# Grouping of destination tiles, and when routed rows are scattered, in a two-layer graph and expert kernel

## The chip, the cores and the metric

The kernel runs on one core of a Trainium2 chip. A core has engines that each work through their own queue of instructions in order: PE (matrix products; its weight loads are listed as PEld), DVE (elementwise and reductions), ACT (elementwise with functions from a table, and copies), POOL (elementwise, and here the issuer of indirect DMAs) and SP (which only issues DMAs). They wait for each other by semaphores. The metric is the time of one execution on the device, in microseconds (us).

## The reference

The input is x, 3125 nodes of 256 features, and 50000 edges sorted by destination. Two layers follow, each a graph step and a mixture of experts, every one on a layernorm of x and added to x:

```
x = x + gnn0(layernorm(x))        # [x, x of one neighbour] @ W.T + b
x = x + experts0(layernorm(x))    # best 2 of 8, relu, hidden 1024
x = x + gnn1(layernorm(x))
x = x + experts1(layernorm(x))    # best 2 of 8, gelu, hidden 256
```

The part that matters here is the second layer. Its graph step is

```
t1  = feat @ W1
msg = (t1[src] + (feat[src] * feat[dst]) @ W2) / sqrt(out_deg[src] * out_deg[dst])
agg = segment_sum(msg, dst)
e   = leaky_relu(where(in_count > 0, t1 + agg, 0) + b, 0.01)
gnn1 = e / max(norm(e), 1e-12)
```

and its experts are, with the two best of a softmax over eight router scores, their weights scaled to sum to one,

```
out = tokens + sum over e of combine[:, e] * (gelu(tokens @ w1[e] + b1[e]) @ w2[e] + b2[e])
```

## The kernel before

Nodes are held in SBUF as T = 25 tiles of 128 rows (the last has 53), in the array X. They are two halves, tiles 0 to 13 and 14 to 24. For the experts, the rows of a half are sent to the sets of their two experts: in half 0 every expert has room for four tiles of rows, in half 1 for three. A set that overflows has extra sets, a branch that does not run here.

**Graph step of layer 1 (to_the_end, L1604 and following).** Edges are turned earlier into 25 tables of counts, one for each destination tile, in memory (atab). The neighbour sums of a group of destination tiles are then a dense product over all 25 source tiles. Groups are listed in `fours`: (0,4), (4,8), (8,12), (12,16), (16,19), (19,22), (22,25). For a group g there is

- `load(t)` (L1615): SP loads the counts of one tile;
- `begin(g)` (L1790): reserves the sums in PSUM, by turns under two names, and transposes the features of the group (turned_rows, L1639 to L1649);
- `product(g, i0, i1)` (L1775): ACT casts the counts from bytes (L1782), PE makes 100 products (L1786), four for each source tile;
- `end(g)` (L1796): two tiles at a time, DVE adds and multiplies the sums with the features (both_rows, L1652 to L1661), and then finish_steps is run for each tile.

**finish_steps (L1664)** makes eight products of a tile with W1 and W2 (L1672), three DVE operations (L1677 to L1679) and a sum of squares on ACT (L1681). The results of several tiles are gathered up to the end of a *span* of up to five tiles: (0,5), (5,10), (10,14), (14,19), (19,24), (24,25). At the last tile of a span come unit_steps (square root on ACT L1578, reciprocal, update of X, L1584) and score_steps (L918): layernorm statistics (L526 to L529), normed rows (L533), which go to `kept` in half 0 and to a buffer `xn5` in half 1, POOL's addition of the normed rows to X (L1588), transposes on PE (L935), a copy on ACT (L937), the router's products (L942), the scores' copy (L944), and for half 1 a store of the rows issued from ACT's queue (L946; the last span from SP's). `xn5` has one buffer; the single tile of the last span has its own, `xn1`. Half 0's last span is followed by route_steps: it ranks the scores, and gives every row its two places in the sets.

**Half 1: place_steps (L1700).** A span of half 1 gets its places as soon as it is scored, from running counts of each set (rank, two small products L1726 and L1727, DVE work), and is scattered to the sets by two indirect DMAs per tile on POOL (L1754). For the span (14,19) this is run in `end`; for the other two it is run beside the experts.

**Half 0: dispatch (L1759).** The rows in `kept` are scattered to the sets (table xtab) by two indirect DMAs per tile on POOL, 28 in all (L1765). It is called for two tiles at a time, after each of the tiles 14 to 20 is finished; ahead of each pair of tiles, DVE copies the places (L1762), and this copy is held in program order:

```
place = state["place"][:, :, t0:t1]
tc.keep_in_program_order(nc.vector.tensor_copy(place, routed2[0].at[:, :, t0:t1]))
```

**Order of the work.** Up to the experts a planner of the framework orders each engine's queue: of what its own cost estimate has ready it takes what is first in the program. A copy held in program order stays behind the DVE instruction traced just before it. The experts (L983) are in an order written out by hand: 16 sets, of which the first eight are half 0's. For each set SP loads the rows (L1037) and the weights (L972 to L980); PE transposes rows (L1061), DVE copies them (L1062); PE makes the hidden layer (L1088), ACT its gelu (L1092); PE makes the outputs (L1102), DVE adds a bias (L1107), POOL scatters them (L1111). The rows of the first two sets are loaded first, then the weights; the rows' load waits for all 28 scatters of half 0, since they write one table. At 11 points of a set of half 0 (10 in half 1), called slots, generators "beside" are moved on by one step. One is `beside_third` (L1830): it finishes and scores the last tile (24), places the spans (19,24) and (24,25), and then routes half 1; only after that are half 1's rows loaded. With finish and score of tile 24 and the two placings, 35 steps stand ahead of that routing.

**Memory.** The buffers of the experts lie where those of the graph step were: the weights of the first sets over the casted counts (`wide`), the transposed rows and the hidden layer over `kept` and over the buffers of route and place; the rows of the second set over a `wide` buffer.

Of the kernel before, what the change touches and what calls it, by code (L numbers as in the profile page):

```python
# [12 lines left out]
I32 = mybir.dt.int32  # L13
# [5 lines left out]
P = 128  # L19
D = 256  # L20
N = 3125
T = (N + P - 1) // P
# [26 lines left out]
HALVES = ((0, 14), (14, T))  # L49
# [31 lines left out]
def groups(n, size, first=0):  # L81
    return [(a, min(a + size, n)) for a in range(first, n, size)]


def run(steps):

    while True:
        try:
            next(steps)
        except StopIteration as end:  # L90
            return end.value
# [19 lines left out]
def gnn_ffn_kernel(ctx: ExitStack, tc: tile.TileContext, x, src_a, src_d, dst_d, dst_row,  # L111
                   gW, gb, fWg, fbg, fW1, fb1, fW2, fb2,
                   hW1, hW2, hb, rW, mw1, mb1, mw2, mb2, out):
    nc = tc.nc
# [7 lines left out]
    def bank(shape, dtype, tag, bufs=2):  # L122
        return psum.tile(shape, dtype, tag=tag, name=tag, bufs=bufs)
# [233 lines left out]
    with tc.tile_pool(name="edges", bufs=2, reuse_waits="tile") as ep:  # L357
# [68 lines left out]
        last = ep.tile([P, 2, T], F32, bufs=1)  # L426
# [66 lines left out]
        last = last[:, 0]  # L493
# [456 lines left out]
    def alone(dma, table, fresh=False):  # L950

        group = f"{table.name}{fresh}"
        tc.declare_no_dep(dma.ins, group=group, reason="other rows of the table")
        tc.add_to_no_dep_group(group, dma.ins)
# [371 lines left out]
    with tc.tile_pool(name="ffn", bufs=2, reuse_waits="tile") as fp:  # L1326
# [7 lines left out]
        with tc.tile_pool(name="gnn", bufs=2, reuse_waits="tile") as gp:  # L1334
# [27 lines left out]
            rp = gp_route.enter_context(tc.tile_pool(name="route", bufs=1, reuse_waits="tile"))  # L1362
# [212 lines left out]
    def unit_steps(emb, sq, t0, t1):  # L1575
        n = t1 - t0
        yield
        nc.scalar.activation(sq[:, :n], sq[:, :n], AF.Sqrt)  # L1578
        yield
        yield  # L1580
        nc.vector.tensor_scalar(sq[:, :n], sq[:, :n], 1e-12, None, OP.max)
        nc.vector.reciprocal(sq[:, :n], sq[:, :n])
        for t in range(t0, t1):
            nc.vector.scalar_tensor_tensor(X[:, t, :], emb[:, t - t0, :], sq[:, t - t0, :],  # L1584
                                           X[:, t, :], OP.mult, OP.add)
# [18 lines left out]
    def to_the_end():  # L1604


        routed2 = [Routed(True, 3, tag=("tr", 2)), Routed(True, by_expert=True)]
# [4 lines left out]
        gp = finishing.enter_context(tc.tile_pool(name="prod", bufs=1, reuse_waits="tile"))  # L1612
        sp = finishing.enter_context(tc.tile_pool(name="score2", bufs=1, reuse_waits="tile"))
        with tc.tile_pool(name="ahead2", bufs=2, reuse_waits="tile") as ap2:
            def load(t):  # L1615
                if t % 8 < 2:
                    at[t] = at[t % 8]
                elif t % 8 < 6:
                    at[t] = ap.tile([P, T, P], U8, name="at")
                else:  # L1620
                    at[t] = ap2.tile([P, T, P], U8, name="at2")
                nc.sync.dma_start(out=at[t].rearrange("p i d -> p (i d)"), in_=atab[t])

            for t in range(2, 8):
# [1 line left out]
                    with tc.tile_pool(name="comb1", bufs=2, reuse_waits="tile") as cp:  # L1626
                        run(combine_and_split(1, cp))
                load(t)
            spans = [g for a, b in HALVES for g in groups(b, 5, a)]
            state = {}  # L1630

            some_deg = gp.tile([P, T], F32, name="some_deg")
# [19 lines left out]
            def both_rows(t0, t1, sums, c0, featT):  # L1652

                n = (t1 - t0) * P if t1 < T else (t1 - t0) * P - P // 2
                both = gp.tile([P, 2, KD, 2 * P], F32, name="both", bufs=2)
                if t1 == T:
                    nc.vector.memset(both[:, :, :, n:n + P // 2], 0.0)
                for k in range(KD):
                    s, f = sums[k][:, c0:c0 + n], featT[:, k].rearrange("p t l -> p (t l)")[:, :n]
                    nc.vector.tensor_add(both[:, 0, k, :n], s, f)  # L1660
                    nc.vector.tensor_mul(both[:, 1, k, :n], s, f)  # L1661
                return both

            def finish_steps(t, both, i):  # L1664
                t0, t1 = next(g for g in spans if g[0] <= t < g[1])
                if t == t0:
                    state["emb"] = gp.tile([P, 5, D], F32, name="emb", bufs=1)
                    state["sq"] = gp.tile([P, 5, 1], F32, name="sq", bufs=2)
                po = bank([P, 2, D], F32, "y")
                for w, Wt in enumerate((hW1t, hW2t)):  # L1670
                    for k in range(KD):
                        nc.tensor.matmul(po[:, w, :], both[:, w, k, i * P:(i + 1) * P], Wt[:, k, :],  # L1672
                                         start=(k == 0), stop=(k == KD - 1))
                yield
                yield
                emb, junk = state["emb"][:, t - t0, :], gp.tile([P, D], F32, name="junk", bufs=2)
                nc.vector.scalar_tensor_tensor(junk, po[:, 1, :], some_deg2[:, t:t + 1], hbt, OP.mult, OP.add)  # L1677
                nc.vector.scalar_tensor_tensor(emb, po[:, 0, :], some_deg[:, t:t + 1], junk, OP.mult, OP.add)
                nc.vector.scalar_tensor_tensor(emb, emb, 0.01, emb, OP.mult, OP.max)  # L1679
                yield  # L1680
                nc.scalar.activation(junk, emb, AF.Square, accum_out=state["sq"][:, t - t0, :])  # L1681
                if t < t1 - 1:
                    return
                yield from unit_steps(state["emb"], state["sq"], t0, t1)
                h = int(t0 >= HALVES[1][0])
                if t0 == HALVES[h][0]:
                    state["pl"] = gp.tile([P, HALVES[0][1], NE], F32, name="pl", bufs=2)
                queue = nc.scalar if t1 < T else nc.sync
                xn = yield from score_steps(sp, h, t0, t1, state["pl"], rWt, tabs2[h][0], plus_normed,
                                            state["kept"][:, t0:t1, :] if h == 0 else None, queue)  # L1690
                if h == 1:
                    due.append((t0, t1, xn))
                if h == 0 and t1 == HALVES[0][1]:
                    with tc.tile_pool(name="route2", bufs=1, reuse_waits="tile") as rp:
                        run(route_steps(routed2[0], rp, 0, state["pl"][:, :HALVES[0][1]], 2))
                    state["place"] = gp.tile([P, 2, t1], I32, name="place")

            due = []

# [58 lines left out]

            def dispatch(t0, t1):  # L1759

                place = state["place"][:, :, t0:t1]
                tc.keep_in_program_order(nc.vector.tensor_copy(place, routed2[0].at[:, :, t0:t1]))  # L1762
                for t in range(t0, t1):
                    for i in range(2):
                        alone(nc.gpsimd.indirect_dma_start(  # L1765
                            out=tabs2[0][0], in_=state["kept"][:, t, :], in_offset=None,
                            out_offset=bass.IndirectOffsetOnAxis(ap=place[:, i, t - t0:t - t0 + 1], axis=0)),
                            tabs2[0][0])

            state["kept"] = ap2.tile([P, HALVES[0][1], D], F32, name="kept", bufs=1)  # L1770
            chunks = [g for a, b in HALVES for g in groups(b, 3, a)]
            fours = groups(16, 4) + groups(T, 3, 16)
            sums, featT = {}, {}

            def product(g, i0, i1):  # L1775
# [20 lines left out]
            def end(g):  # L1796
                t0, t1 = fours[g]
                for a, b in groups(t1, 2, t0):
                    both = both_rows(a, b, sums[g], (a - t0) * P, featT[a])
                    for t in range(a, b):  # L1800
                        if t == T - 1:
                            return both
                        run(finish_steps(t, both, t - a))
                        if due and t < T - 2:
                            with tc.tile_pool(name="place", bufs=1, reuse_waits="tile") as rp:
                                run(place_steps(rp, *due.pop()))
                        first = 2 * (t - HALVES[1][0])
                        if 0 <= first < HALVES[0][1]:
                            dispatch(first, first + 2)

            begin(0)
            begin(1)
            product(0, *HALVES[0])
            product(1, *HALVES[0])
            product(0, *HALVES[1])
            end(0)
            product(1, *HALVES[1])
            end(1)
            for g in range(2, len(fours)):
                for t in range(*fours[g]):  # L1820
                    if t >= 8:
                        load(t)
                begin(g)
                product(g, 0, T)
                last = end(g)

        aheads.close()
        fp = aheads.enter_context(tc.tile_pool(name="ffn2", bufs=3, side="right", reuse_waits="tile"))

        def beside_third():  # L1830
            yield from finish_steps(T - 1, last, 0)
            with tc.tile_pool(name="place", bufs=1, reuse_waits="tile") as rp:
                for one in due:
                    yield from place_steps(rp, *one)
            finishing.close()
            with tc.tile_pool(name="route3", bufs=1, reuse_waits="tile") as rp:
                yield from route_steps(routed2[1], rp, 1, None, 2, state["scores"])
# [319 lines left out]
```

## Time and profile before

| what | us |
|---|---|
| median of three runs | 1002.73 |
| the three runs | 1002.85, 1001.3, 1002.73 |
| profiled execution | 999.52 |
| its span, first to last instruction | 997.7 |
| last product L1786 ends | 812.8 |
| first expert product L1088 starts | 844.53 |
| third expert's L1088 starts | 869.79 |

The profile is of one execution. Its span lies between the first and the last instruction of the engines; the mean granted clock of PE over it is 0.957 of full speed. It lists, in this order: busy time of each engine with its share of the span and its number of instructions; busy tenths in forty slices (24.9 us each); DMA queues; the chain that ended last; the groups of instructions that cost most; DMA issues. A trace behind it can be asked for busy times in any stretch, and for one engine's timeline: start, duration, engine and line, operation, output<-inputs, shapes, count, and in brackets how long the engine had stood idle before, and on whose work. The costliest lines of the page in the second layer:

```
L1786 PE MATMUL sa<-wide,parts 128*128 128x512 f32 (+2 forms) x200 | 72.4, 365 | 2.4 <-ACT wide L1782 2.4
L1786 PE MATMUL big<-wide,parts 128*128 128x512 f32 (+1 forms) x300 | 71.7, 387 | 0.3 <-ACT wide L1782 0.3
L1786 PE MATMUL sb<-wide,parts 128*128 128x512 f32 (+2 forms) x200 | 71.9, 363 | 0.0
L1782 ACT CAST wide<-at 128x384 fp32r<-128x384 uint8 (+1 forms) x225 | 95.0, 485 | 42.0 <-PE sb L1786 21.5
```

A line of a group has the number of instructions, their busy time in us and the mean ns of one, and then the idle time of the engine just before them and what ended most of it. Busy times of PE overlap, since products are pipelined: from start to start a 512-wide product of L1786 takes 0.215 us.

### The profile page before, as it was taken

Reading aid. Unit: us, or ns where it says so; the run is one execution under the profiler, and the core shown is the slowest. Engines: PE = TensorE matmul, PEld = TensorE weight load, DVE = VectorE, ACT = ScalarE, POOL = GpSimd, SP = SyncE. Lnnn points to the kernel's source line nnn. Section 1 sums busy time; section 2 is a strip of 40 time slices with the busy share of each in tenths; the row PEclk is TensorE's granted clock in tenths of the full one; section 3 lists DMA queues with packets and bytes.
Section 4 is the critical chain, followed back from the end, with each engine's and each line's share of the span. In section 5 each row is a group of like instructions: output and inputs, shape, how many; then the busy total and the mean of one; then the engine's idle time right before and its main releaser. Section 6 shows DMA issues by size and latency. Waiting matters only on the chain. (4 is left out here: it accounts for less than half of the span.)

```text
span 997.7 us, 13976 instructions
## 1 busy us (share of the span) xinstructions
PE 875.3 (88%) x4819; PEld 653.5 (66%) x4819; DVE 595.2 (60%) x1585; ACT 413.1 (41%) x970; POOL 332.9 (33%) x338
## 2 busy tenths in 40 slices
PE   4778579998999999999999998899999974799880
PEld 3666446664766576777777776778889963566660
DVE  8966883773555555665566307452648771685553
ACT  2872421221126655666632236655455630412110
POOL 1356446432642332133221110000112554376450
PEclk9999889999999999999999999899999995999995
DMA  8785574542537675656566404111021215566975
GB/s 230 240 244 151 152 225 143 171 141 73 166 84 269 201 264 199 214 192 231 179 210 215 165 21 146 66 67 66 1 67 39 90 69 191 176 200 212 299 247 176
DMA packets 121576, 161.99 MB, mean 162 GB/s; under 512 B 20324, under 2 KB 97614, under 8 KB 121375
## 3 DMA queue, kind: packets, MB, share of 16 engines
q1 hardware_dynamic: 99459, 113.97, 36.3%
q0 software_dynamic: 13200, 34.14, 10.1%
q10 hardware_dynamic: 8836, 12.89, 3.6%
q8 instruction: 40, 0.66, 0.3%
q14 instruction: 41, 0.34, 0.1%
HBM read 98.06 MB, written 64.27 MB: 163 GB/s over the span
## 5 line engine op out<-in xcount | busy, mean ns | idle before, releaser
L1102 PE MATMUL y<-w,hid 128*128 128x256 f32 (+2 forms) x1120 | 268.6, 385 | 10.4 <-DVE y L1107 6.0
L1088 PE MATMUL big<-xs,w 128*128 128x488 f32 (+1 forms) x640 | 268.0, 542 | 0.7 <-ACT hid L1092 0.5
L1102 PEld LDWEIGHTS y<-w,hid 128*128 128x128 f32 (+2 forms) x1120 | 197.8, 185 | 41.1 <-DVE y L1107 8.4
L1111 POOL DMA_INDIRECT ytab<-y,put x112 | 128.7, 1149 | 224.7 <-DVE y L1107 191.5
L1092 ACT ACTIVATE hid<-big,bt 128x488 f32<-128x488 f32 (+1 forms) x160 | 98.7, 617 | 219.5 <-PE big L1088 207.0
L1088 PEld LDWEIGHTS big<-xs,w 128*128 128x128 f32 x640 | 112.2, 192 | 60.5 <-issue 35.3
L1107 DVE TENSOR_TENSOR y<-y,b2t 128x256 f32<-128x256 f32 (+1 forms) x112 | 47.2, 423 | 111.0 <-PE y L1102 110.7
L1782 ACT CAST wide<-at 128x384 fp32r<-128x384 uint8 (+1 forms) x225 | 95.0, 485 | 42.0 <-PE sb L1786 21.5
L1042 POOL DMA_INDIRECT g<-xtab,take x56 | 60.5, 1080 | 145.7 <-PE tr L1061 110.3
L1308 PEld LDWEIGHTS <-hq 128*128 128x128 bf16 x800 | 57.2, 98 | 58.4 <-issue 38.6
L1288 DVE TENSOR_TENSOR hq<-qs,iota_b 128x2048 bf16<-128x2048 bf16 x50 | 61.1, 1222 | 52.2 <-PE sb L1308 52.2
L1786 PE MATMUL sa<-wide,parts 128*128 128x512 f32 (+2 forms) x200 | 72.4, 365 | 2.4 <-ACT wide L1782 2.4
L1786 PE MATMUL big<-wide,parts 128*128 128x512 f32 (+1 forms) x300 | 71.7, 387 | 0.3 <-ACT wide L1782 0.3
L1786 PE MATMUL sb<-wide,parts 128*128 128x512 f32 (+2 forms) x200 | 71.9, 363 | 0.0
L1309 ACT CAST at<-sa 128x400 uint8<-128x400 f32 x100 | 49.1, 491 | 47.8 <-PE sa L1308 46.7
L1062 DVE COPY xs<-tr 128x488 f32<-128x488 f32 (+1 forms) x64 | 35.7, 598 | 48.1 <-PE tr L1061 47.8
L1309 ACT CAST at<-sb 128x400 uint8<-128x400 f32 x100 | 49.0, 490 | 29.3 <-PE sb L1308 27.9
L1786 PEld LDWEIGHTS big<-wide,parts 128*128 128x128 f32 x300 | 55.0, 192 | 8.3 <-ACT wide L1782 1.1
L1588 POOL TENSOR_TENSOR X<-X,kept 128x256 f32<-128x256 f32 x14 | 10.4, 773 | 139.1 <-DVE kept L533 139.1
L1291 DVE TENSOR_TENSOR hc<-cs,iota_b 128x1600 bf16<-128x1600 bf16 x50 | 49.2, 985 | 0.0
L1152 DVE SCALAR_TENSOR_TENSOR X<-y,weight,X 128x256 f32<-128x256 f32 (+1 forms) x78 | 35.5, 479 | 13.6 <-DMA y<-ytab 12.6
L1786 PEld LDWEIGHTS sa<-wide,parts 128*128 128x128 f32 x200 | 37.6, 188 | 6.8 <-ACT wide L1782 2.8
(370 smaller groups left out, 1242.0 us busy)
## 6 DMA issues: line engine op xcount, KB each, us to landing
w<-in_fW SPq DMA_DIRECT2D x32, 1024.0 KB
ytab<-zero_b SPq DMA_DIRECT2D x10, 1024.0 KB
atab<-at ACTq DMA_DIRECT2D x25, 400.0 KB
at<-atab SPq DMA_DIRECT2D x25, 400.0 KB
y<-ytab SPq DMA_DIRECT2D x19, 512.0 KB
w<-in_mw SPq DMA_DIRECT2D x32, 256.0 KB
xtab<-zero_b SPq DMA_DIRECT2D x7, 1024.0 KB
rows<-xtab SPq DMA_DIRECT2D x8, 512.0 KB
```

Of the source, the lines that this page charges most:

```text
L1042: nc.gpsimd.indirect_dma_start(out=g, out_offset=None, in_=tabs[h][0], in_offset=bass.IndirectOffsetOnAxis(ap=routed[h].column(c)[0], axis=0))
L1088: nc.tensor.matmul(ph[:, :many], w1[:, i, c * P:(c + 1) * P], turned[k][:, i, :many], start=(i == 0), stop=(i == KD - 1))
L1092: nc.scalar.activation(hid[:, c, :many], ph[:, :many], act, bias=bt[:, 0, c:c + 1])
L1102: nc.tensor.matmul(py[:m], hid[:, c, j * P:j * P + m], w2[:, c, :], start=(c == 0), stop=(c == nh - 1))
L1107: nc.vector.tensor_add(y[:m], py[:m], b2t[:m])
L1111: dma = nc.gpsimd.indirect_dma_start(out=tabs[h][1], out_offset=into, in_=y[:m], in_offset=None, bounds_check=2 * tokens(h) - 1, oob_is_er ...
L1288: nc.vector.tensor_tensor(in_pairs(hq), pairs(qs[:, mine], P), in_pairs(iota_b[:, None, :].to_broadcast([P, n, P])), OP.is_equal)
L1291: nc.vector.tensor_tensor(in_pairs(hc), pairs(cs[:, mine], C), in_pairs(iota_b[:, None, :C].to_broadcast([P, n, C])), OP.is_equal)
L1308: nc.tensor.matmul(pa[:, j], hq[:, g + j, :], hc[:, g + j, :], start=True, stop=True)
L1309: nc.scalar.copy(at[:, :, W * (g0 + g):W * (g0 + g + 4)].rearrange("p i (g w) -> p i g w", w=W), pa.rearrange("p g i w -> p i g w"))
L1782: nc.scalar.copy(wide[:, :j1 - j0, t - t0, :], at[t][:, j0:j1])
L1786: nc.tensor.matmul(sums[g][d][:, :n], parts[:, i, k, d * P:(d + 1) * P], wide[:, i - j0].rearrange("p t l -> p (t l)")[:, :n], start=(i == ...
```

## The change

The groups are (0,4), (4,8), (8,11), (11,14), (14,18), (18,22), (22,25): a group ends where the first half ends. The spans are the same groups. Dispatch is called once, right after the first half is routed: one copy of all places, not held in program order, and 28 indirect DMAs behind each other. `end` becomes a generator. It places a group of half 1 as soon as the group is finished: (14,18) and (18,22) ahead of the experts, by 16 scatters. The last group's `end`, with the sums' additions, the finishing and the scoring of three tiles, is moved on beside the experts, and then its placing with six scatters; 31 steps stand ahead of half 1's routing. What `load`, `begin` and `product` do is unchanged, and so are the experts.

```diff
-            spans = [g for a, b in HALVES for g in groups(b, 5, a)]
+            fours = [(0, 4), (4, 8), (8, 11), (11, 14), (14, 18), (18, 22), (22, T)]
...
             def finish_steps(t, both, i):
-                t0, t1 = next(g for g in spans if g[0] <= t < g[1])
+                t0, t1 = next(g for g in fours if g[0] <= t < g[1])
...
                         run(route_steps(routed2[0], rp, 0, state["pl"][:, :HALVES[0][1]], 2))
-                    state["place"] = gp.tile([P, 2, t1], I32, name="place")
+                    dispatch(0, t1)
...
             def dispatch(t0, t1):
 
-                place = state["place"][:, :, t0:t1]
-                tc.keep_in_program_order(nc.vector.tensor_copy(place, routed2[0].at[:, :, t0:t1]))
+                place = gp.tile([P, 2, t1 - t0], I32, name="place")
+                nc.vector.tensor_copy(place, routed2[0].at[:, :, t0:t1])
                 for t in range(t0, t1):
...
-            fours = groups(16, 4) + groups(T, 3, 16)
...
                     both = both_rows(a, b, sums[g], (a - t0) * P, featT[a])
                     for t in range(a, b):
-                        if t == T - 1:
-                            return both
-                        run(finish_steps(t, both, t - a))
-                        if due and t < T - 2:
-                            with tc.tile_pool(name="place", bufs=1, reuse_waits="tile") as rp:
-                                run(place_steps(rp, *due.pop()))
-                        first = 2 * (t - HALVES[1][0])
-                        if 0 <= first < HALVES[0][1]:
-                            dispatch(first, first + 2)
+                        yield from finish_steps(t, both, t - a)
+                if due and g < len(fours) - 1:
+                    with tc.tile_pool(name="place", bufs=1, reuse_waits="tile") as rp:
+                        yield from place_steps(rp, *due.pop())
...
-            end(0)
+            run(end(0))
             product(1, *HALVES[1])
-            end(1)
+            run(end(1))
...
                 product(g, 0, T)
-                last = end(g)
+                if g < len(fours) - 1:
+                    run(end(g))
...
         def beside_third():
-            yield from finish_steps(T - 1, last, 0)
+            yield from end(len(fours) - 1)
```

## The prediction

> **What bounds the kernel now.** I read busy times by engine first, then forty slices, then stretches around the change, and last, per engine, what each instruction waited for. From the page:
>
> ```profile
> PE 875.3 (88%) x4819; PEld 653.5 (66%) x4819; DVE 595.2 (60%) x1585; ACT 413.1 (41%) x970; POOL 332.9 (33%) x338
> ...
> PE   4778579998999999999999998899999974799880
> PEclk9999889999999999999999999899999995999995
> ```
>
> TensorE (PE) is the bound, 88% busy, and nearly full up to the hole "74" (slices 33 and 34, 798 to 848 us), where its clock also falls. Stretches around it (us; busy time of PE, PEld, DVE, ACT, POOL; granted clock; DMA share; GB/s):
>
> ```profile
> 786.50:812.50 26.00, 25.43 (x171) 23.63 (x169) 17.67 (x69) 14.02 (x36) 9.87 (x12) 1.00 0.15 57
> 812.50:830.00 17.50, 8.18 (x37) 6.56 (x35) 11.23 (x38) 2.11 (x7) 13.23 (x15) 0.72 0.25 99
> 830.00:844.50 14.50, 4.26 (x20) 3.98 (x20) 0.87 (x2) 0.86 (x2) 6.27 (x8) 0.50 0.56 189
> ```
>
> The products end at 812.8 with PE 98% busy; the first expert matmul (L1088) starts at 844.53; between, PE does 12.4 us of work at a clock of 0.72 and 0.50. The timelines of PE, ACT, SP and POOL say why:
>
> ```profile
> 825.40 1.94 PE L935 MATMUL tr<-ident,xn 128*128 128x128 f32 x8 [8.44 <-DVE xn L533]
> ...
> 840.24 1.88 PE L942 MATMUL y<-rWt,hT 128*128 128x8 f32 x8 [10.68 <-ACT hT L937]
> ```
> ```profile
> 839.61 0.86 ACT L937 COPY hT<-tr 128x512 f32<-128x512 f32 x2 [12.49 <-DMA rows<-xtab]
> ```
> ```profile
> 834.98 0.92 SPq L1037 DMA_DIRECT2D rows<-xtab  x2
> ```
> ```profile
> 765.79 1.49 POOL L1765 DMA_INDIRECT xtab<-kept,place  x1 [17.79 <-DVE qb L832]
> ...
> 785.94 0.98 POOL L1765 DMA_INDIRECT xtab<-kept,place  x1 [0.30 <-issue]
> ...
> 805.25 0.98 POOL L1765 DMA_INDIRECT xtab<-kept,place  x1 [11.36 <-DVE place L1762]
> ...
> 807.82 1.11 POOL L1754 DMA_INDIRECT ytab<-xn,toi  x1 [0.30 <-DVE junk L1677]
> ...
> 820.99 0.98 POOL L1765 DMA_INDIRECT xtab<-kept,place  x1 [0.30 <-DMA ytab<-xn,toi]
> ...
> 832.48 0.97 POOL L1765 DMA_INDIRECT xtab<-kept,place  x1 [0.30 <-issue]
> ```
>
> Bottom up: 16 of the 28 scatters of the first half (L1765) run by 787. The last twelve come in twos behind pinned copies (L1762); ten stand behind the ten scatters of the second half (L1754) and end at 833.46. The rows of the first two experts are loaded at 834.98, land by 839.2, and ACT and PE wait for that. The third expert starts its L1088 at 869.79, 57.0 after the products. The profiled execution took 999.52 (span 997.7 and 1.8 around it), 3.2 under the median 1002.73; I sum in it and carry the difference over.
>
> **Part by part.**
>
> Regrouping: the seven widths are the same set (4,4,4,4,3,3,2.5 tiles), so products, casts and finishing cost the same in sum: 0. It is covered by nothing, but it is equal. The order shifts: (11,14) ends two tile widths earlier (100 matmuls of 0.215 for four tiles, 5.4 per tile), so the first half's product ends at 732.5 - 10.8 - 1.75 (one finishing less) = 720 instead of 732.5. Scores followed 17.5 later (pl copy 750.0) and places 15 after that (at, 764.96): places at about 752.5.
>
> Scatter at once: removes six pinned copies (0.17 each on DVE) and puts 28 scatters in a row on POOL. Their pace is 0.97 + 0.30 = 1.28 us (767.59 to 785.94), 28 x 1.28 = 36: 752.5 to 788.5, landed 2.4 later, 24 before the products end. Behind them on POOL stand the residual adds L1588, needed much later, and the eight L1754 scatters of (14,18), ready at about 785 to 790: 8 x 1.29 more, free by 801. What hides it: POOL is otherwise 9.9 of 26 busy there. DMA share there is 0.15. How fast can POOL issue while DVE works? With DVE 79% busy (13.05 of 16.5 us, 769.5 to 786) the 16 scatters held 1.28, the worst took 1.49. Bounds: 28 x 1.28 = 36 and 28 x (1.49 + 0.30) = 50, end 788.5 to 802.5; I take 36, the mean of 16 rows. Either is before the products end, so the rows' load is no longer late. What is late next is weights: expert 0's w1 lies where the last wide tile was, freed by the last product matmul.
>
> [...]
>
> Products' end: before, 19 tiles were scored by then, now 22 (three spans of four, and all of the first half); finishing is 22 tiles in both. Score rows L935 + L942 sum to 13.4 for 19 tiles, 0.7 a tile, and 1.0 by busy time: +2.5 for three (bounds 0, if they fall into gaps, and 3.0). End: 812.8 + 2.5 = 815.3.
>
> First expert matmul: before, the transposes of the rows and DVE's copies took 841.97 to 844.53 = 2.6 (at half clock). w1 waits for the last product; an SP load takes about 1 us to start and 0.7 for 256 KB at the 370 KB/us of the rows. So at least +1.7. The upper end: DVE and PE, in order, may still be placing (18,22): scores of a four-tile group come 17.5 to 26 after its product (750.0 - 732.5; 795.4 - 769.4), here 790 + 17.5 to 26 = 807.5 to 816, and places 10 later (795.4 to 805.3): up to 826, +11. The planner can put the experts' transposes ahead of that, as it did at 841.97 between two L942 blocks. I take +4.5, nearer the low end for that reason: 819.8, against 844.53.
>
> From there to the third expert it was 25.3. Added: finishing of 22 and 23 on PE, 2 x 1.75 = 3.5 (before in the hole); score of two more tiles, 2 x 0.8 = 1.6; PE waits for the two both_rows blocks on DVE in the hand-written order, 0.8 and 1.5 (four adds of 0.41 and four of 0.21) = 2.3; the chain emb, square, sqrt, X, statistics, sqrt, normed of three tiles instead of one, which held ACT and so expert 1's second gelu: 3.04 + 0.68 before, 4.6 to 6 now: +2; DVE shared with placing (18,22): +2 (0 to 4); finishing, scores and y add in one PSUM name of two buffers: +1 (0 to 2). Subtracted: no half clock (844.5 to 848 at 0.59): -0.8; the five-tile placing with ten scatters is gone from here, three tiles and six remain: -0.5. One pair of table switches (2 x 1.28 on ACT) goes too, already in the chain. Sum 25.3 + 12.4 - 1.3 = 36.4; third expert at 819.8 + 36.4 = 856.2 against 869.8: 13.6 saved.
>
> Clock: it fell to 0.50 after PE had waited 8.44, and stayed 1.00 through the wait of 3.04 at 852; a wait of 4.6 to 6 lies between. If it falls, at most half of 4 us: +2. [...]
>
> Later: routing of the second half is four slots earlier (31 steps before it for 35), but its rows are not asked for before the ninth set. From the third expert to the end, 128 us, nothing is touched: 0; PE and DMA bound that (DMA share 0.92 to 1.01 in 920 to 960).
>
> **Rivals.**
>
> A, bigger: the added finishing and scoring fall into waits PE has anyway in the first two experts (5.1 us at 851 to 869; and 2.3 + 2 + 1 of mine vanish), and the first expert starts at 817: gain 22 to 27, 976 to 981. For: those waits. Against: they are tied to the same chain on ACT and DVE.
>
> B, smaller: placing (18,22) does stand ahead of the first expert (start at 826), or normed of (22,25) waits for its one buffer (xn5 is read by the eight L1754 scatters of (18,22), issued 826 to 836, landing 839), stopping DVE's in-order queue and so the expert's copies. 826 + 34 = 860 at the best, 866 with 6 of wait: gain 4 to 10, 993 to 999. For: one buffer, place chain of 10. Against: normed comes some 18 after the first expert's start.
>
> C, slower: places come late because DVE is crowded, so the burst starts late, and with one xn5 buffer the eight scatters of (14,18) behind 28 hold the normed of (18,22); DVE being in order, finishing and then the score transposes on PE stop inside the products, which nothing covers. Expected release 803, needed at about 800 to 805. PE can meanwhile do what is left of the last group's product (14.7 in all; I estimate 8). So it decides from a burst start of 752.5 + 13.6 + 8 = 774; at 782 it ends 8 above before: 1002.7 + 8 = 1011 (1005 to 1015). For: at (the places) came 15 after the scores with DVE at 29.1 of 33 (755 to 788). Against: PE was never held over 0.5 there.
>
> D, nothing: the rows' load is early but the start stays where it was, by weights or the score chain: 1001 to 1004. Against: w1 is a 256 KB load that SP, free by then, issues at once, and the score chain's waits were those for the rows.
>
> **How the numbers follow.** Mine 0.56 (1002.73 - 13.6 = 989.1; its own range 984 to 993); A 0.14; B 0.17; C 0.10; D 0.03. Faster 0.56 + 0.14 + 0.17 = 0.87, same 0.03 (0.2% is 2 us; the three runs span 1.5), slower 0.10. The range takes A's and B's bounds, 976 to 1000, and leaves out C, D and a little of A.
>
> **What would show it.** Right: 28 L1765 in one row from about 752 to 789; the load L1037 issued before the products end; ACT not waiting for rows; first L1088 at 817 to 823; third expert's at 853 to 860; finishing L1672 of three tiles among L1088/L1102; the clock at 1.00 through 812 to 845. Wrong: PE waits of more than 2 us before 812 (C), a DVE wait for ytab<-xn,toi ahead of L533 (B), the first L1088 after 826 (B), L1765 at over 1.8 us apiece.

## The result

On the chip of the first comparison the changed kernel took 988.72 us (median of four, 987.86 to 993.17) for 1002.01 of the kernel before: a ratio of 0.9881, with a 95% interval of 0.9845 to 0.9917. The prediction was 989.1, with a range of 976 to 1000. The experiments ran on three chips, called A, B and C, on which both kernels are some 6% slower and the gain of the change is smaller; that is told with the experiments. The chip of the first comparison ("first" below) is not named in its results, so that it is a fourth one is concluded from its times alone.

The profiled execution of the changed kernel took 988.86, its span 987.1. Its busy times and forty slices, in the form shown for before:

```profile
PE 882.5 (89%) x4819; PEld 655.8 (66%) x4819; DVE 599.6 (61%) x1583; ACT 410.9 (42%) x969; POOL 334.1 (34%) x338
...
PE   4788469998999999999999999899999998889990
PEclk9989879999999999999999999899999999799995
```

The hole of PE before the experts ("74" in the slices of before) is gone. A "7" in the clock, slice 35, is new. Stretches around the experts' start (us; busy PE, PEld, DVE, ACT, POOL; granted clock; DMA share; GB/s): from the products' end to the first expert product, from there to the third expert, and the part of that in which the clock falls:

```profile
822.70:825.70 3.00, 0.84 (x9) 0.64 (x7) 2.62 (x7) 0.00 (x0) 2.03 (x3) 1.00 0.55 132
825.70:860.10 34.40, 28.44 (x106) 20.28 (x107) 15.96 (x45) 9.19 (x17) 14.05 (x15) 0.85 0.61 196
...
844.00:862.00 18.00, 14.49 (x51) 10.41 (x50) 9.42 (x29) 3.73 (x7) 5.39 (x7) 0.72 0.36 104
```

POOL's timeline has the 28 scatters of the first half in one row, and SP's the load of the first rows right behind it (the 24.80 beside it are the wait of the second set's load for its buffer, a wide tile, not for the scatters):

```profile
756.18 1.06 POOL L1765 DMA_INDIRECT xtab<-kept,place  x1 [16.64 <-DVE qb L832]
...
791.72 0.97 POOL L1765 DMA_INDIRECT xtab<-kept,place  x1 [0.30 <-issue]
...
798.16 1.01 POOL L1754 DMA_INDIRECT ytab<-xn,toi  x1 [2.50 <-DVE toi L1750]
```
```profile
794.28 24.80 SPq L1037 DMA_DIRECT2D rows<-xtab  x2
822.77 0.37 SPq L972 DMA_DIRECT2D w<-in_mw  x1
```

PE's timeline has what came in the hole's place:

```profile
825.72 1.06 PE L1088 MATMUL big<-xs,w 128*128 128x488 f32 x2 [2.17 <-DVE both L1661]
...
834.92 1.13 PE L1672 MATMUL y<-hW1t,both 128*128 128x256 f32 x4 [1.40 <-DVE both L1660]
...
848.14 0.67 PE L935 MATMUL tr<-ident,xn 128*128 128x128 f32 x4 [2.90 <-DVE xn L533]
...
860.10 2.62 PE L1088 MATMUL big<-xs,w 128*128 128x488 f32 x6
```

The 2.17 of the first of these lines is put down to a DVE addition that ends as the product starts. The weights of the first expert, which the product also waits for, landed at 825.58, and two other profiles below put the same wait, of 2.11 and 2.14, down to that load.

The two profiled executions differ by 5.0 already ahead of the change: the first transposes of features (L1647) start at 626.35 and 631.39, and up to there PE runs the same instructions in the same order. So I count from that point. Times between marks, in us (first to second, products' end to the first expert product, first to third expert, third expert to the end of the span), for every profile of this study:

| kernel | chip | L1647 to products' end | to first expert | first to third expert | to the end |
|---|---|---|---|---|---|
| before | first | 186.5 | 31.7 | 25.3 | 127.9 |
| whole change | first | 191.3 | 3.0 | 34.4 | 127.0 |
| scatter alone | A | 208.8 | 26.9 | 25.4 | 144.5 |
| groups alone | A | 211.5 | 2.9 | 37.3 | 137.9 |
| last group first | A | 218.2 | 21.5 | 21.4 | 131.1 |
| whole + four slots | A | 218.3 | 3.0 | 31.5 | 140.3 |
| whole change | B | 215.6 | 3.0 | 37.4 | 135.4 |
| scatter alone | B | 212.6 | 27.5 | 24.8 | 145.1 |
| whole + four slots | B | 215.5 | 3.0 | 31.5 | 138.6 |
| groups alone | B | 211.4 | 3.0 | 37.3 | 138.9 |
| before | C | 189.0 | 39.0 | 27.5 | 147.4 |
| pairs + four slots | C | 207.0 | 3.0 | 30.5 | 138.4 |
| pairs + slots, later transposes | C | 206.9 | 3.0 | 30.1 | 138.1 |
| whole change | C | 215.1 | 3.0 | 36.1 | 135.0 |

On the first chip the way from L1647 to the third expert goes from 243.4 to 228.7: 14.7 saved. Behind it 0.9 more is saved, and 5.0 is lost ahead of it, where the two kernels do the same: 14.7 + 0.9 - 5.0 = 10.6, the difference of the two spans (997.7 and 987.1).

### The profile page after: what moved, and what is told of

Its sections match the earlier page's. It is cut to its first block, busy times and chain, and to the rows that moved or that the text cites. A ratio compares the mean times of both kernels' runs of the same rounds, so it can differ in the third digit from the quotient of the medians.

```text
span 987.1 us, 13968 instructions
## 1 busy us (share of the span) xinstructions
PE 882.5 (89%) x4819; PEld 655.8 (66%) x4819; DVE 599.6 (61%) x1583; ACT 410.9 (42%) x969; POOL 334.1 (34%) x338
## 3 DMA queue, kind: packets, MB, share of 16 engines
q0 software_dynamic: 13200, 34.14, 10.2%
## 5 line engine op out<-in xcount | busy, mean ns | idle before, releaser
L1102 PE MATMUL y<-w,hid 128*128 128x256 f32 (+2 forms) x1120 | 274.4, 391 | 6.2 <-DVE y L1107 5.9
L1102 PEld LDWEIGHTS y<-w,hid 128*128 128x128 f32 (+2 forms) x1120 | 201.0, 189 | 38.5 <-DVE y L1107 9.2
L1785 PE MATMUL big<-wide,parts 128*128 128x512 f32 (+1 forms) x300 | 74.2, 390 | 0.3 <-ACT wide L1781 0.3
```

The source lines that it names most:

```text
L1102: nc.tensor.matmul(py[:m], hid[:, c, j * P:j * P + m], w2[:, c, :], start=(c == 0), stop=(c == nh - 1))
L1785: nc.tensor.matmul(sums[g][d][:, :n], parts[:, i, k, d * P:(d + 1) * P], wide[:, i - j0].rearrange("p t l -> p (t l)")[:, :n], start=(i == ...
```

## Experiments

All kernels of one set ran on one chip, beside runs of the kernel before; none ran on the first chip, so what each part gives there is concluded from these. Before took 1066.45 on chip A, 1077.68 on B and 1067.55 on C. Some 38 to 47 us of that are lost ahead of the products: L1647 starts at 669.6 to 673.5 in all twelve profiles, for 626.35 and 631.39 on the first chip.

### The scatter in one row, without the new groups

```diff
-                    state["place"] = gp.tile([P, 2, t1], I32, name="place")
+                    dispatch(0, t1)
...
-                place = state["place"][:, :, t0:t1]
-                tc.keep_in_program_order(nc.vector.tensor_copy(place, routed2[0].at[:, :, t0:t1]))
+                place = gp.tile([P, 2, t1 - t0], I32, name="place")
+                nc.vector.tensor_copy(place, routed2[0].at[:, :, t0:t1])
...
-                        first = 2 * (t - HALVES[1][0])
-                        if 0 <= first < HALVES[0][1]:
-                            dispatch(first, first + 2)
```

Chip A:

> The kernel before (old groups, old spans, last tile alone beside the experts) with one thing of the change: the 28 scatters of the first half in a row as soon as that half is routed, from one copy of the places. Theory A (the late rows held ACT and PE, so the scatter carries most of the gain): L1765 in one row from about 766 to 802, the load of the rows issued before 812, ACT without its 12.5 us wait for rows, first expert product L1088 at 826 to 832 in place of 844.5, time 984 to 990. Theory B (the regrouping and the deferred last group carry most of it): the score chain of (19,24) still holds PE until about 840, time 996 to 1002.

It took 1077.18: ratio 1.0096 (1.0052 to 1.0140), slower than before, which neither theory had. The rows were in time: SP issued their load at 847.20, the products ended at 881.6, and ACT's copies of the scoring no longer wait for rows. But PE kept waiting for the score chain, as theory B says. PE, from the products' end on:

```profile
885.09 2.93 PE L1672 MATMUL y<-hW1t,both 128*128 128x256 f32 x6 [3.48 <-issue]
...
900.20 2.39 PE L935 MATMUL tr<-ident,xn 128*128 128x128 f32 x8 [8.43 <-DVE xn L533]
902.38 1.71 PE L942 MATMUL y<-rWt,hT 128*128 128x8 f32 x8
...
908.54 2.00 PE L1088 MATMUL big<-xs,w 128*128 128x488 f32 x2
```

The wait of 10.68 behind ACT is gone. The 8.4 for the normed rows of (19,24) stand as before, and so, by an estimate from eight products of L942 (1.71 here; before, 1.88 at a clock of 0.50 and 0.95 at full clock), does the half clock. The hole is 26.9 long, of which 3.5 is a stand that the profile gives to no one ("issue"); the kernel before has 31.7 on the first chip and 39.0 on chip C. And the products, with 208.8, are about 20 longer than those of before on the first chip and on chip C. Inside them PE stood several times, the longest for 5.3 (up to 832.5), while POOL issued the row.

Repeated on chip B. Theory C was set up after the first set: a long row of scatters from POOL leaves the other engines without instructions.

> The kernel before with the 28 scatters in one row alone, once more. From its first profile (first expert product 26.9 after the products, of which 3.5 a stall for instructions, in place of 31.7) theory A says now: 7 to 9 saved in the hole and nothing else, ratio 0.990 to 0.993 on a chip without the stalls. Theory C on a chip with them: ratio 1.005 to 1.015, as measured (1.0096).

It was 1081.15, ratio 1.0036 (1.0010 to 1.0063): slower again, a little less than theory C had. The scatter alone shortens the hole, but on these chips it doesn't pay.

### The new groups, with the scatters in held pairs

```diff
-                    dispatch(0, t1)
+                    state["place"] = gp.tile([P, 2, t1], I32, name="place")
...
-                place = gp.tile([P, 2, t1 - t0], I32, name="place")
-                nc.vector.tensor_copy(place, routed2[0].at[:, :, t0:t1])
+                place = state["place"][:, :, t0:t1]
+                tc.keep_in_program_order(nc.vector.tensor_copy(place, routed2[0].at[:, :, t0:t1]))
...
                         yield from finish_steps(t, both, t - a)
+                        first = 2 * (t - HALVES[1][0])
+                        if 0 <= first < HALVES[0][1]:
+                            dispatch(first, first + 2)
```

> The changed groups and the last group beside the experts, but the scatters of the first half as before: seven pairs of tiles, each behind a copy of its places held in program order after tiles 14 to 20. Theory A: the last six pairs of scatters stand behind the eight of the placing of (14,18) and end at about 815 to 823, the rows are loaded then and land 4 to 5 later, first L1088 some 3 to 8 later than with the whole change, time 992 to 997. Theory B (regrouping carries it): 987 to 990, as the whole change. If the scatter is everything and regrouping costs: 1000 or more.

It took 1057.34: ratio 0.9893 (0.9842 to 0.9945). My theory was wrong here. Tile 20, behind which the last pair hangs, is in the group (18,22) now, and that is finished ahead of the last product. The last scatter was issued at 860.11, 21.8 ahead of the products' end (881.90), and the first expert starts 2.9 after that end, as with the whole change:

```profile
860.11 0.97 POOL L1765 DMA_INDIRECT xtab<-kept,place  x1 [0.30 <-issue]
```
```profile
884.85 1.97 PE L1088 MATMUL big<-xs,w 128*128 128x488 f32 x2 [2.11 <-DMA w<-in_mw]
```

So the new groups, with the last one beside the experts, cure the late rows without the scatter in one row. On chip B:

> The changed groups with the scatters in held pairs, once more. Its first profile has the rows in time (first expert 2.9 after the products, last of the 28 scatters 21 before it), so the scatter in one row should add nothing to the groups: equal to the whole change within 2 us on a chip without stalls; on a chip with them 5 to 12 faster than the whole change, since the longest row is twelve scatters instead of 28.

It took 1063.22, ratio 0.9879 (0.9838 to 0.9920), 4.6 less than the whole change in the same set (1067.77, 0.9936 with 0.9904 to 0.9968). That is just short of the 5 to 12 expected for a chip with stalls. The two intervals overlap, so this pair alone doesn't rank them.

### The last group ahead of the experts

```diff
                 product(g, 0, T)
-                if g < len(fours) - 1:
-                    run(end(g))
+                run(end(g))
...
         def beside_third():
-            yield from end(len(fours) - 1)
```

> The whole change, but the last group (tiles 22 to 24) is finished and scored ahead of the experts; only its placing is beside them. Theory A: PE stands again between the products and the first expert while DVE and ACT go through the chain of the last group (finishing 5, chain 9, scoring 3 to 5), first L1088 about 20 after the products in place of 3, the first two experts shorter by 10 to 12, time 992 to 996. Rival (deferring costs in the experts what it saves ahead of them): 987 to 990.

It took 1064.14: ratio 0.9974 (0.9939 to 1.0009). The hole is back: 21.5 from the products' end to the first expert, of which 9.5 is one wait:

```profile
903.29 1.65 PE L935 MATMUL tr<-ident,xn 128*128 128x128 f32 x6 [9.49 <-DVE xn L533]
```

But the first two experts take 21.4 in place of 36 to 37. Added up, 42.9 against 39.1 to 40.4 of the whole change on chips C and B: putting the last group beside the experts saves 18.5 ahead of them and gives 15 to 16 back in them. Both theories were half right. The 3 that remain are gone further on: behind the third expert this version takes 131.1 and the whole change 135.0 and 135.4, so that from the products' end to the end of the span it is 174.0 against 174.2 and 175.8. With one profile each, on different chips, a gain from putting the last group beside the experts is not shown on A to C.

### Four slots more ahead of the last group's statistics

```diff
                 yield from unit_steps(state["emb"], state["sq"], t0, t1)
+                for _ in range(4 if t1 == T else 0):
+                    yield
```

> The whole change with four more steps of waiting between the update of X and the statistics of the last group, so that the second square root comes to ACT behind both gelus of the second expert, and the scoring's transposes come to PE behind its output products. Theory A (the order written by hand makes ACT and PE wait there, 845.2 to 848.1 in the changed kernel, and the clock is at 0.50 from 848.9 to 859 because of that): no stall of 2.9, the clock stays at 1.00, third expert at 853 to 857 in place of 860.1, time 982 to 986. Rival 1: the stall comes back at the next expert with the scoring, clock falls there, 987 to 990. Rival 2: the clock falls anyhow (it is not that stall), 986 to 989.

It took 1060.56: ratio 0.9940 (0.9914 to 0.9965). From the first to the third expert it took 31.4, and ACT had both gelus of the second expert behind it before the second square root:

```profile
914.22 1.25 ACT L1092 ACTIVATE hid<-big,bt 128x488 f32<-128x488 f32 x2
915.49 1.28 ACT L528 ACT_TABLE_LOAD   x1
916.79 0.30 ACT L528 ACTIVATE mvx<-mvx,eps 128x3 f32<-128x3 f32 x1
```

The whole change was not in this set, so a second set had both, on chip B:

> The whole change with four more steps of waiting ahead of the last group's statistics, once more, beside the whole change. From its first profile, third expert 31.4 after the first in place of 34.4: theory A says 2 to 4 less than the whole change on the same chip. Rival (given back with the next expert's scoring, where a wait of 2.4 came up): no difference from the whole change, within 2.

> The whole change once more, beside the parts, so that all stand on the same chip. On the chip of the first comparison it took 988.7 for 1002.0 (0.988). On the chip of the first experiments, where the engines stood some 20 us without instructions inside the products while POOL issued a long row of scatters, theory C (a long row of scatters from POOL starves the other engines of instructions there) gives it a stall of 12 to 25 us at 756 to 793 of its own row, and a ratio of 0.995 to 1.005; if the stall has nothing to do with the row, the ratio is again 0.985 to 0.991 on any chip.

With four slots 1059.02, ratio 0.9842 (0.9799 to 0.9886); the whole change 1067.77, 0.9936 (0.9904 to 0.9968): 8.8 less, more than expected, and the intervals do not touch. In the profiles, 5.9 of it is between the first and the third expert (37.4 and 31.5); 3.2 of that is given back further on, so that the profiles don't account for all 8.8. The clock there, for the whole change and with four slots:

```profile
910.00:915.00 5.00, 2.10 (x7) 0.90 (x6) 4.14 (x15) 1.77 (x3) 1.10 (x2) 0.94 0.52 152
915.00:920.00 5.00, 5.00 (x24) 4.69 (x23) 1.84 (x3) 2.01 (x4) 1.78 (x3) 0.50 0.17 41
920.00:925.00 5.00, 4.48 (x13) 3.23 (x13) 1.29 (x5) 0.00 (x0) 1.47 (x2) 0.50 0.50 169
925.00:930.00 5.00, 5.00 (x13) 3.13 (x12) 2.69 (x11) 0.19 (x1) 1.51 (x2) 0.70 0.30 85
```
```profile
915.00:920.00 5.00, 5.00 (x19) 4.32 (x20) 1.08 (x3) 0.00 (x0) 3.81 (x5) 0.58 0.28 82
920.00:925.00 5.00, 5.00 (x14) 2.41 (x13) 1.48 (x6) 2.32 (x3) 1.03 (x1) 0.74 0.56 169
925.00:930.00 5.00, 4.86 (x28) 3.88 (x27) 4.38 (x20) 0.67 (x1) 1.62 (x2) 1.00 0.60 180
```

The fall of the clock is shorter, not gone. That this stand in the experts costs time is shown on chip B; how much of it is the stand and how much the clock is not separated.

### Both together, and before on the same chip

Pairs and four slots are the two edits above on the changed kernel. "Later transposes" has two more steps between the normed rows and the scoring's transposes of the last group:

```diff
...
+        for _ in range(2 if t1 == T and h == 1 and beside_too else 0):
+            yield
         ps = bank([P, t1 - t0, NE], F32, "y")
...
```

Chip C:

> The kernel before itself, profiled on the chip of these runs. Theory C (long rows of scatters leave the other engines without instructions on such a chip): its 16 scatters in a row stand inside the products and its 20 in a row after them, so 0 to 12 us of stall inside the products, less than with 28 in a row; from the first feature transposes to the products' end 187 to 200 (186.5 on the first chip). If such a chip stalls in the products anyhow: 205 to 220, as in the others.

> The changed groups with the scatters in held pairs, and the four steps of waiting ahead of the last group's statistics. Theory A adds the two: third expert 31 to 32 after the first (37.4 with the pairs alone), and where long rows stall, fewer stalls than with 28 in a row: 3 to 6 less than the whole change with four steps, ratio to before 0.975 to 0.983 on a chip as the last two, 0.980 to 0.986 on one as the first. Rival (the two share what they save): as the better of the two, 0.984 to 0.988.

> The same with two more steps between the normed rows and the scoring's transposes of the last group. With four steps PE still stood 1.9 for the normed rows at the second expert and the clock fell to 0.50 for 6 us behind it. Theory A (the stand is what lowers the clock): no stand, the clock stays at 1.00, 2 to 4 less than with four steps. Rival: the transposes come into the next expert and make it wait there, no difference within 2.

> The whole change a third time, beside the others. Ratio to before 0.985 to 0.991 on a chip without the stalls, 0.990 to 0.997 on one with them (0.9936 was measured).

| kernel | median us | ratio to before | 95% interval |
|---|---|---|---|
| whole change | 1066.60 | 0.9996 | 0.9972 to 1.0020 |
| pairs + four slots | 1049.98 | 0.9835 | 0.9796 to 0.9875 |
| pairs + slots, later transposes | 1048.90 | 0.9807 | 0.9768 to 0.9847 |

The whole change made no measurable difference on this chip, outside what I expected of it. The two versions with pairs and slots are 16.6 and 17.7 faster than it, beyond the better of the two edits alone (8.8, on chip B), though just past the slow end of the 0.975 to 0.983 that I had written for the first. The later transposes bring 1.1, within noise, as the rival said: PE no longer stands for the normed rows, but stands 2.82 at the same expert's outputs (L1104 in that kernel, behind DVE's addition), and the clock falls there, for 3.4 instead of 6.8. Neither version was run on a chip like the first.

The one execution of before (1078.01, some 10 above the median of its chip) stalls hardly at all in the products: 189.0 from L1647 to their end, inside the 187 to 200 of theory C, where the whole change takes 215.1 and 215.6. Its hole, in which its last 22 scatters stand in one row, is 39.0 instead of 31.7. The stretch of the row of 28, for the changed kernel on the first chip and on chip C, from the start of the row to its end:

```profile
756.00:793.00 37.00, 36.29 (x200) 28.76 (x200) 27.01 (x116) 20.39 (x52) 27.98 (x29) 1.00 0.28 111
```
```profile
794.00:831.00 37.00, 23.70 (x111) 16.43 (x110) 14.63 (x69) 6.85 (x19) 27.32 (x28) 0.87 0.24 98
```

POOL does the same in both, at the same pace (1.32 and 1.31 apiece). On chip C PE is busy for two thirds, DVE for half and ACT for a third of the time of the first chip. PE there, in the middle of a product, waits for nothing that the profile knows, one matmul at a time:

```profile
824.62 0.58 PE L1785 MATMUL big<-wide,parts 128*128 128x512 f32 x1 [1.70 <-issue]
826.71 0.59 PE L1785 MATMUL big<-wide,parts 128*128 128x512 f32 x1 [1.51 <-issue]
828.12 0.58 PE L1785 MATMUL big<-wide,parts 128*128 128x512 f32 x1 [0.82 <-issue]
```

and ACT's casts stand 14.47 for "remote", which stands for a semaphore's rise that the profile can give to no instruction:

```profile
829.58 1.01 ACT L1781 CAST wide<-at 128x256 fp32r<-128x256 uint8 x3 [14.47 <-remote]
```

Set against the length of the row inside the products (one execution each, chips A, B and C): two rows of eight with 3.5 between them and the first six of the last row, 189.0; a row of 20 (eight of L1754 and twelve of L1765), 206.9 to 211.5; 28 in a row, 208.8 and 212.6 in the old groups, 215.1 to 218.3 in the new ones. So theory C's pattern holds, and pairs are the better choice on such chips. But number goes with length: inside the products lie 22 scatters of before and 34 to 36 of all others. Pairs and the whole change have the same 36 there, the pairs with two more pauses of 3.2 to 5.7, and differ by 4 to 8; the other 18 to 22 above before can be the number of scatters as well as the length of the row.

That the engines lack instructions was my reading of "issue", and the traces speak against it at the stands that can be followed. They hold the times at which semaphores rise, beside the views. In both profiles of the first chip, up to the last 0.5 us of the span, every rise of PE's own semaphore (1610 before, 1608 with the change) lies within 0.05 us of the end of a PE instruction that makes it, and no engine's wait is put down to "remote". Each of the four profiles of chip A has 11 to 21 such waits, the longest of 20.0 or 20.1. ACT's 14.47 on chip C is one, and POOL issued scatters through all of it (815.11 to 829.58). One of 12.33 ahead of ACT's casts, in the groups alone on chip B, ended at 867.34, 2.9 behind a row of scatters, and PE then stood 10.16 for the cast. The "issue" stand of 3.48 of the scatter alone lies behind a third: the last product ended at 881.61 by the profile, DVE's addition, which waits for it, began at 884.61 after 7.38 of "remote", with POOL issuing throughout, and PE's next product began at 885.09. So there PE stands behind DVE or ACT, and these behind a rise that no recorded work accounts for. Whether that signal is late or the product itself ends later than the profile has it (ends of products are modelled), why POOL's scatters go with it, and whether all stands are of this kind, stays open.

## Why the prediction was right, and where its working failed

The number was right within 0.4 us, and the mechanism in its outline: the hole before the experts closes, the finishing and scoring of the last group come into the experts, the rest stays. Counted from L1647 on the first chip, 14.7 was saved where the sum said 13.6. That the number came so near is luck in part: three terms of the sum were off by 2.3 one way and by 1.5 and 2.0 the other, and in the two profiles 5.0 was lost ahead of the change. Its steps:

- **Places and scatters.** Predicted from 752.5 to 788.5 at 1.28 apiece; measured 756.18 to 792.69, and (791.72 - 756.18) / 27 = 1.32 apiece. With the 5.0 of the start taken off, the row began 1.4 earlier than predicted. DVE was 27.0 of 37 busy beside it, and no scatter of the row took more than 1.12 or stood more than 0.48 behind the one before. So beside a busy DVE the row stayed within 0.04 of the 1.28 apiece.
- **"DMAs late" as the cause.** The step "last twelve scatters stand behind the ten of the second half" described before rightly, but not what cures it. Groups alone start the first expert as early as the whole change does, with pairs still held. The row of 28 is not needed for the gain, and the scatter alone leaves a hole of 26.9. What failed is the sentence under rival D that the score chain's waits were those for the rows: with the rows in time PE still stood 8.43 for the normed rows, as it had stood 8.44. This wait went because the last group's scoring was moved beside the experts; with it ahead of them PE stood 9.49.
- **Products' end, +2.5.** Measured 191.3 - 186.5 = +4.8. The three more scored tiles cost 2.5 (L935 and L942 are busy for 19.4 in place of 17.0), as priced. The other half are waits inside the products (4.2 in place of 1.8), the longest 1.5 of PE for DVE's both_rows. I had left PE's waits at those of before.
- **First expert, +4.5.** Measured 3.0, of which 2.17 is the wait for the weights. The start, 825.72, is past the 817 to 823 named in the prediction, and inside it (820.7) with the 5.0 of the start taken off. The placing of (18,22) did stand ahead of the experts, as rival B says, but DVE was through with it at 822.8, with the products: my 826 was the far end of its bounds.
- **First to third expert, 36.4.** Measured 34.4 on the first chip, 36.1 and 37.4 on C and B. The waits that I priced are there: both_rows 1.40, normed rows 2.90. The clock is where a size was wrong: "at most +2", half of 4 us, a length that was only my estimate. It was at 0.50 for 10.2 us, from 848.9 to 859.1, in which PE was busy for 9.6; products of L1102 start 0.427 apart there and 0.216 apart at full clock, so by an estimate from these the work would take half as long, some 4.8 less, apart from what would have turned into waits. The terms for DVE and for the bank of two must have been smaller to make up for it; they were not measured apart.
- **Rival B's one buffer, and C.** The normed rows of (18,22) waited 0.33 for a DVE result (811.23), not for the scatters of (14,18). The buffer held nothing up on the first chip.
- **Behind the third expert, 0.** 127.9 and 127.0.

What none of my cases had is the loss inside the products on the other chips. There the change's ratio was 0.9936 and 0.9996. Rival C named the place (a stop inside the products from the row of scatters), but by another mechanism, the xn buffer, for which none of the stands followed above waited.

## What to carry to other kernels

When a stall has two causes, one behind the other, ask which of them still stands when the other goes: here taking away the late rows alone left the score chain, and regrouping with the last group beside the experts removed both. Work that was moved beside a hand-ordered stage was not free there; of 18.5 saved ahead of the experts 15 to 16 came back in them and, by the profiles of chips A to C, the rest behind them; four more steps of delay won part of it back (37.4 to 31.5 there, on chip B). In the new groups the products took 215.1 to 218.3 on chips A to C with an unbroken row of 28 indirect DMAs on one queue, and 206.9 to 211.5 with held pairs; so try the broken row beside it, and on more than one chip. When a profile gives a stand to no one, compare the time at which the semaphore rose with the end of the work that raises it.

## What the runs showed of the hardware

- The same program took 1002 us on one chip and 1066 to 1078 on three others, with POOL's scatter pace the same (1.28 to 1.32 us). Inside a row of 28 scatters PE was busy 36.3 of 37 us on the first and 23.7 of 37 on another.
- On chips A to C, DVE and ACT waited for a semaphore's rise that no recorded work accounts for: 7.38 (scatter alone, A), 12.33 (groups alone, B) and 14.47 (whole change, C), each while POOL issued indirect DMAs or until 2.9 behind them. In the two profiles of the first chip there is no such wait, and up to the last 0.5 us every rise of PE's semaphore lies within 0.05 us of the end of the work that makes it.
- PE's clock went to 0.50 after a stand of 2.90 (845.2 to 848.1 in the changed kernel), while it had stayed at 1.00 through one of 3.04 in the kernel before, also in the first two experts. With pairs and four slots it fell behind a stand of only 1.53:

```profile
855.51 1.56 PE L1102 MATMUL y<-w,hid 128*128 128x256 f32 x6 [3.04 <-ACT hid L1092]
```
```profile
904.88 0.67 PE L935 MATMUL tr<-ident,xn 128*128 128x128 f32 x4 [1.53 <-DVE xn L533]
```
```profile
905.00:910.00 5.00, 4.37 (x18) 3.36 (x17) 2.30 (x6) 0.59 (x1) 4.24 (x6) 0.69 0.12 43
```

So a stand's length alone doesn't say whether the clock falls. More can be read from the times of the clock's changes, which the traces hold: in the two of the first chip they lie 3.41 us or a multiple of it apart. Cut into windows of 3.41 us on that grid, from the first change to the last, the two profiles have 22 windows at full clock in which PE was busy for at most 0.48, and the clock was at half in the next window behind 18 of them; of the 490 others it was so behind one. The stand of 2.90 fell into one window (845.4 to 848.9, PE busy 0.21 of it). The longer one of 3.04 was cut in two by the end of a window (0.50 and 0.46). The one of 1.53, on chip C, ended at 904.88, the clock fell at about 906.9, and in the 3.41 us before that fall PE was busy for 0.41 of the time. So the clock fell also behind windows in which PE was at work for up to 0.48 of the time.
